# Splitting half B's recurrent matmuls by output columns in an LSTM step

## The chip, the cores and the metric

The kernel runs on one core of a Trainium2 chip. The metric is the time of one execution on the device, in microseconds (us); before the change it is 1897.9 us, the median of 3 runs (1897.48 to 1903.74). About 0.5% is what a measurement of this kernel can tell from no change.

## What is computed

`x` has 8 sequences of 512 steps with 512 features. An LSTM with 512 hidden units is run over it and added to `x`; a convolution over 8 steps, two projections, a linear scan with 64 states and a last projection are run over that sum and added again.

```python
def step(carry, xw_t):                  # xw_t = x[:, t] @ Wx + b
    prev_h, prev_c = carry
    a = xw_t + prev_h @ Wh              # 8 x 2048: gates i, f, o, g
    next_c = sigmoid(f) * prev_c + sigmoid(i) * tanh(g)
    next_h = sigmoid(o) * tanh(next_c)
    return (next_h, next_c), next_h
```

The 512 steps depend on each other, so the time is close to 512 times that of one step.

## The kernel before

**Matmuls (PE).** The 512 hidden units are four chunks of 128. The moving operand is a weight matrix, as a high and a low float16 part (`whh`, `whl` for Wh, `wxh`, `wxl` for Wx); the stationary operand is the state (`stat`, 16 or 32 columns) or the input (`xs`). The outputs are halves: A (output chunks 0 and 1) and B (chunks 2 and 3), each with PSUM tiles `hp[h]` of 128 x 256. Columns 0 to 191 hold gates g, i and f, columns 192 to 255 gate o. One "group" below is the 4 matmuls (L314, q = 0 to 3) of one half, one input chunk and one weight part; they go to four column tiles of the array. A step has 16 such groups. Their order is written out by hand, as (half, input chunk):

```python
PE_ORDER = ((0, 0), (0, 1), (1, 0), (0, 2), (0, 3), (1, 1), (1, 2), (1, 3))
```

Behind them stand the bias (one group, L296) and x's part (`x_mm`, 8 groups, L304) for half t % 2 of the next pair of steps, in another buffer; then at most one or a few float32 matmuls of the second layer, `pl` and `pl2` (L492, L501, L536), from a queue of filler work. Chunks 0 and 1 of `stat` come from half A of the step before, chunks 2 and 3 from half B.

**The order of the rest** is written by hand too. A letter is an operation, the letter after it a half:

```python
ORDER = "TA tA aA gA bA TB vA oA aB gB cA tB kA pA bB oB vB iA mA cB lA kB pB iB mB lB f q E"
```

- `T` (L569, VectorE, "DVE"): long transpose of columns 0 to 191 of `hp` into `Z`. `t` (L572, DVE): short transpose of columns 192 to 255 into `Zo`.
- `a` (L576, DVE): adds the parts of Z into `zp`. `b` (L581, GpSimd, "POOL"): adds the parts of Zo into `zo`.
- `g` (L585, ScalarE, "ACT"): tanh of g, i, f. `o` (L588, ACT): tanh of o, from `zo`.
- `v` (L591), `c` (L595), DVE: the new cell. `k` (L598), `p` (L601), ACT: its tanh and a copy.
- `i` (L604), `m` (L607), `l` (L610), DVE: the new `stat`, high and low part; `l` is what the next step's matmuls wait for.
- `f`: fillers of the second layer on DVE, up to a planned cost FILL = 0.8 a step. `q`: in odd steps a one-column copy on ACT (L657). `E`: fillers on ACT and POOL.

TA is thus the long transpose of half A, lB the last DVE operation of half B. Each engine takes its instructions in this order. `Zo` and `zo` have 4 buffers for each half; a buffer is written again four steps later, and the write has to come after the earlier reads of it: tB after bB of four steps ago (POOL), bB after oB of four steps ago (ACT).

Of the kernel before, what the change touches and what calls it, by code (L numbers as in the profile page):

```python
# [9 lines left out]
F32 = mybir.dt.float32  # L10
# [9 lines left out]
EXP1 = float(1 << 23)  # L20
FMAX = 65504.0

ORDER = "TA tA aA gA bA TB vA oA aB gB cA tB kA pA bB oB vB iA mA cB lA kB pB iB mB lB f q E"

PE_ORDER = ((0, 0), (0, 1), (1, 0), (0, 2), (0, 3), (1, 1), (1, 2), (1, 3))
DUMMY = 4
FILL = 0.8
TAILD = 14
# [62 lines left out]
def lstm_conv_ssm_kernel(ctx: ExitStack, tc: tile.TileContext, xT, condT, wx, wh, brow, cbp, wpp, bpp,  # L91
                         wsp, bsp, alogp, dtlogp, wop, bop, outT):
    nc = tc.nc
    T = xT.shape[2]
# [4 lines left out]
    v, s, pe, sp = nc.vector, nc.scalar, nc.tensor, nc.sync  # L99

    cp = ctx.enter_context(tc.tile_pool(name="cp", bufs=1))
# [5 lines left out]
    wb = [[cp.tile([128, 4, 4, 512], F16, name=f"w{m}{p}") for p in "hl"] for m in "hx"]  # L107
# [3 lines left out]
    def carve(slot, off, shape, parts=128):  # L111
        n = 1
        for d in shape:
            n *= d
        a = wraw[0:parts, slot, off:off + n]
        if len(shape) == 2:
            a = a.rearrange("p (a b) -> p a b", a=shape[0])
        elif len(shape) == 3:
            a = a.rearrange("p (a b c) -> p a b c", a=shape[0], b=shape[1])
        return a  # L120
# [9 lines left out]
    def load_x(n, t0=0, t1=BLK):  # L130
        if n < NBLK:
            sp.dma_start(xbuf[n % 4][:, :, t0 * NB:t1 * NB],
                         xT[:, :, n * BLK + t0:n * BLK + t1, :].rearrange("p k t b -> p k (t b)"))

    seen = cp.tile([128, 1], F32, name="seen")
    v.memset(seen, 0.0)
    s.activation(seen, seen, AF.Tanh)

    seq = [(0, 0), (1, 0), (1, 1), (1, 2), (1, 3), (0, 1), (0, 2), (0, 3)]
# [24 lines left out]
    hp = [[t[:, 0:256] for t in r] for r in hpb]  # L164
# [4 lines left out]
    pool = nc.gpsimd  # L169
# [123 lines left out]
    def bias_mm(P, h):  # L293

        for q in range(4):
            pe.matmul(hp[h][P % 2][32 * q:32 * q + 32, :], bst[P > 0][:, q], bmov[:, 256 * h:256 * h + 256],  # L296
                      start=True, stop=False, tile_position=(0, 32 * q), skip_group_check=True)

    def x_mm(P, h, ks):
        S = xs[P // (BLK // 2) % 2]  # L300
        for k in ks:
            for W in wb[1]:
                for q in range(4):
                    pe.matmul(hp[h][P % 2][32 * q:32 * q + 32, :], S[:, k, P % (BLK // 2)],  # L304
                              W[:, k, q, 256 * h:256 * h + 256],
                              start=False, stop=False, tile_position=(0, 32 * q), skip_group_check=True)

    def h_mm(t, h, ks):
        S = stat[t % 2]
        o = 16 * (t % 2)  # L310
        for k in ks:
            for wi, W in enumerate(wb[0]):
                for q in range(4):
                    pe.matmul(hp[h][(t // 2) % 2][32 * q:32 * q + o + 16, :], S[:, k, 0:o + 16],  # L314
                              W[:, k, q, 256 * h:256 * h + 256],
                              start=False, stop=(k == 3 and wi == 1),
                              tile_position=(0, 32 * q), skip_group_check=True)


# [26 lines left out]
                                  op=ALU.mult),  # L346
# [55 lines left out]
        bias_mm(0, h)  # L402
    for c, (m, k) in enumerate(seq):
        for h in range(2):
            x_mm(0, h, (k,)) if m else h_mm(0, h, (k,))

    cv = carve(0, 0, (4, NT))
    e, w, x = (carve(0, 1024 + 256 * i, (NT,), 64) for i in range(3))
    lt = [[carve(1, 1024 * i + 256 * j, (NT,), 64) for j in range(4)] + [carve(2, 1024 * i, (4, NT))] for i in range(2)]
    fl = Filler(fps)  # L410
# [18 lines left out]
    def add_x(n, t0=0, after=-1):  # L429
        for k in range(4):  # L430
            src, tmp, dst = x_parts(n, k, t0)
            sx = SX[:, k:k + 1]
            a = fl.add("po", lambda k=k, src=src, tmp=tmp: nc.gpsimd.tensor_scalar(
                tmp, src, CL[:, 0, k:k + 1], CL[:, 1, k:k + 1], op0=ALU.min, op1=ALU.max),
                deps=(xlast.get((n - 1, k)),), after=after)
            a = fl.add("xa", lambda sx=sx, tmp=tmp, dst=dst: s.activation(dst[0], tmp, AF.Copy, scale=sx),
                       deps=(a,), after=after)
            xlast[n, k] = fl.add("xd", lambda sx=sx, tmp=tmp, dst=dst: v.scalar_tensor_tensor(
                dst[1], tmp, sx, dst[0], op0=ALU.mult, op1=ALU.subtract), deps=(a,), after=after, cost=0.4)
# [180 lines left out]
    for t in range(T):  # L620
        n, r = divmod(t, BLK)
        if r == 0:
            assert all(h["x2"] in fl.done for h, (b0, *_) in zip(hist, l1blocks) if b0 < t - BLK)
            load_x(n + 2)
            if n + 1 < NBLK:
                add_x(n + 1, 0, t)
        if nl1 < len(l1blocks) and l1blocks[nl1][0] + l1blocks[nl1][1] <= t:
            add_l1(nl1, *l1blocks[nl1])
            nl1 += 1
        if t:  # L630
            for h, k in PE_ORDER:
                h_mm(t, h, (k,))

        P = t // 2 + 1
        if 2 * P < T:
            assert P < 6 or all( xlast[2 * P // BLK, k] in fl.done for k in range(4))
            bias_mm(P, t % 2)
            x_mm(P, t % 2, range(4))
        room = (1 if t < T - 32 else 3) if 2 * P < T else 4
        while room > 0:  # L640
            cost = fl.pop("pl2", t) or fl.pop("pl", t)
            room -= cost
            if not cost:
                break
        ch = {"A": Chain(t, 0), "B": Chain(t, 1)}
        for op in ORDER.split():
            if op == "f":
                left = FILL
                while True:
                    got = fl.pop("xd", t, left) or fl.pop("d2", t, left) or fl.pop("dve", t, left)  # L650
                    left -= got
                    if not got:
                        break
            elif op == "q":

                if t % 2:
                    s.activation(seen, ch["B"].tc[:, 0:1], AF.Copy)  # L657
            elif op == "E":
                for _ in range(2):
                    fl.pop("xa", t) or fl.pop("al2", t) or fl.pop("al", t)  # L660
                fl.pop("po", t)
            else:
                getattr(ch[op[1]], "o_" if op[0] == "o" else op[0])()
        fl.pop("sp", t)
# [69 lines left out]
```

## Time and profile before

| | us |
|---|---|
| median of 3 runs | 1897.9 |
| the profiled execution | 1898.87 |
| its span, first to last instruction | 1897.1 |
| first TA to last TB (L569) | 41.0 to 1859.1 |
| busy: PE, DVE, ACT, POOL | 1653.8, 1648.8, 782.2, 288.2 |
| granted TensorE clock, mean | 0.992 |

Columns of a timeline line: start in us, length in us, engine, line of the kernel, operation, output and input tiles, shape of output and input (for a matmul stationary, then moving operand), number of instructions merged into the line, and in brackets how long the engine had been idle and what ended that. PEld is the load of a stationary operand. A group line has busy time, mean length of one in ns, and idle time ahead of it with its causes. A matmul's length includes the way through the array; matmuls that follow each other start closer than that.

### The profile page before, as it was taken

The numbers are of one execution on the slowest core, as the hardware profiler recorded it, in microseconds if no ns is written. First come the engines' busy times: TensorE is split into PE (matmuls) and PEld (weight loads), VectorE is DVE, ScalarE is ACT, GpSimd is POOL, SyncE is SP. The second block draws the span as 40 slices with busy tenths as digits, with TensorE's granted clock in tenths as the row PEclk, the third lists the DMA queues.
The fourth block names the chain that finished last, engine by engine and source line by source line (L and its number), as shares of the span: only waits on it lengthen the run. The fifth ranks groups of instructions, "written<-read, shape, count | busy, mean of one in ns | idle before, by whom it ended". The sixth has DMA issues, their size and how long they took to land.

```text
span 1897.1 us, 119869 instructions
## 1 busy us (share of the span) xinstructions
PE 1653.8 (87%) x51861; PEld 1364.6 (72%) x51861; DVE 1648.8 (87%) x9137; ACT 782.2 (41%) x4684; POOL 288.2 (15%) x1110
## 2 busy tenths in 40 slices
PE   6888898898988889898898988889898898988896
PEld 4777777777777777777777777777776777777786
DVE  8778889898898989889898898989889898898984
ACT  5544344344434444443444434434443344434342
POOL 1211111111111111111111111111111111111110
PEclk9999999999999999999999999999999999999997
DMA  6000000000000000000000000000000000000000
GB/s 237 4 4 15 4 26 4 4 27 4 26 4 4 27 4 26 4 26 4 4 27 4 26 4 5 26 4 27 4 26 4 4 15 4 15 4 15 4 13 15
DMA packets 21428, 33.52 MB, mean 18 GB/s; under 512 B 2592, under 2 KB 19616, under 8 KB 19872
## 3 DMA queue, kind: packets, MB, share of 16 engines
q1 hardware_dynamic: 20656, 25.71, 4.0%
q8 instruction: 405, 6.64, 1.5%
q14 instruction: 127, 1.04, 0.2%
q10 hardware_dynamic: 240, 0.13, 0.0%
HBM read 17.45 MB, written 8.39 MB: 14 GB/s over the span
## 4 chain that ended last, share of the span: by engine, by line
DVE 50%; PE 31%; ACT 11%; POOL 4%; issue 4%; DMA 0%; ACTq 0%; POOLq 0%; DVEq 0%
PE hp L314 20%; DVE Z L569 16%; DVE wraw L480 7%; DVE zp L576 6%; PE hp L304 5%; ACT gate L585 5%; POOL zo L581 4%; DVE stat L610 3%; DVE stat L604 3%; ACT gate L588 3%; PE fps L501 3%; DVE u L591 3%; DVE Zo L572 3%; ACT tc L598 3%; DVE hb L607 2%
## 5 line engine op out<-in xcount | busy, mean ns | idle before, releaser
L314 PE MATMUL hp<-whh,stat 128*16 128x256 f16 (+1 forms) x16384 | 932.8, 274 | 212.8 <-DVE stat L610 208.4
L314 PEld LDWEIGHTS <-stat 128*16 128x16 f16 x32768 | 777.2, 93 | 443.8 <-DVE stat L610 374.2
L314 PE MATMUL hp<-whl,stat 128*16 128x256 f16 (+1 forms) x16384 | 928.9, 273 | 0.2 <-DVE whl L279 0.2
L585 ACT ACTIVATE gate<-zp 128x48 f32<-128x48 f32 x1022 | 216.2, 212 | 906.1 <-DVE zp L576 903.6
L569 DVE STREAM_TRANSPOSE Z<-hp 128x192 f32<-128x192 f32 x1024 | 391.6, 382 | 111.7 <-PE hp L314 98.4
L304 PE MATMUL hp<-wxh,xs 128*32 128x256 f16 x8192 | 481.6, 273 | 5.5 <-DVE xs L354 5.5
L581 POOL TENSOR_TENSOR zo<-Zo 128x16 f32<-128x16 f32 x1024 | 245.1, 239 | 1571.5 <-DVE zp L576 1092.4
L304 PE MATMUL hp<-wxl,xs 128*32 128x256 f16 x8192 | 481.6, 273 | 0.0
L304 PEld LDWEIGHTS <-xs 128*32 128x32 f16 x16384 | 438.9, 97 | 15.4 <-DVE xs L354 5.7
L588 ACT ACTIVATE gate<-zo 128x16 f32<-128x16 f32 x1022 | 220.6, 216 | 158.1 <-POOL zo L581 141.6
L604 DVE SCALAR_TENSOR_TENSOR stat<-gate,tc 128x16 f16<-128x16 f32 x1024 | 179.5, 175 | 69.0 <-ACT tc L598 0.6
L572 DVE STREAM_TRANSPOSE Zo<-hp 128x64 f32<-128x64 f32 x1024 | 229.9, 225 | 0.0
L576 DVE TENSOR_TENSOR zp<-Z 128x48 f32<-128x48 f32 x1024 | 211.2, 206 | 0.0
L610 DVE TENSOR_TENSOR stat<-hb,stat 128x16 f16<-128x16 f32 x1024 | 179.3, 175 | 17.5
L591 DVE SCALAR_TENSOR_TENSOR u<-gate 128x32 f32<-128x32 f32 x1024 | 175.9, 172 | 20.9 <-ACT tc L598 0.2
L480 DVE SCALAR_TENSOR_TENSOR wraw<-x2b,cond,wraw 128x256 f32<-128x256 f32 (+1 forms) x434 | 188.7, 472 | 4.7 <-ACT wraw L483 4.7
L601 ACT ACTIVATE gate<-zp 128x16 f32<-128x16 f32 x1024 | 188.5, 184 | 0.0
L607 DVE SCALAR_TENSOR_TENSOR hb<-gate,tc 128x16 f32<-128x16 f32 x1024 | 186.3, 182 | 0.0
L598 ACT ACTIVATE tc<-zp 128x16 f32<-128x16 f32 x1024 | 185.2, 181 | 0.4 <-DVE zp L595 0.2
L595 DVE SCALAR_TENSOR_TENSOR zp<-u 128x16 f32<-128x16 f32 x1024 | 177.3, 173 | 0.0
L296 PE MATMUL hp<-bmov,bst 128*32 128x256 f16 x2048 | 144.5, 273 | 0.0
L296 PEld LDWEIGHTS <-bst 128*32 128x32 f16 x2048 | 54.7, 97 | 3.2 <-issue 0.3
(121 smaller groups left out, 739.2 us busy)
## 6 DMA issues: line engine op xcount, KB each, us to landing
x<-in_xT_dram SPq DMA_DIRECT2D x15, 512.0 KB, 4.0
out_dram<-wraw SPq DMA_DIRECT2D x15, 512.0 KB, 4.1
wraw<-in_wh_dram SPq DMA_DIRECT2D x4, 1024.0 KB, 13.7
wraw<-in_wx_dram SPq DMA_DIRECT2D x4, 1024.0 KB, 10.9
x<-in_xT_dram SPq DMA_DIRECT2D x2, 256.0 KB, 12.9
wp<-in_wp_dram SPq DMA_DIRECT2D x1, 256.0 KB, 7.1
out_dram<-wraw SPq DMA_DIRECT2D x1, 256.0 KB, 2.8
out_dram<-wraw SPq DMA_DIRECT2D x2, 128.0 KB, 2.2
```

Source lines behind the costliest of these rows:

```text
L304: pe.matmul(hp[h][P % 2][32 * q:32 * q + 32, :], S[:, k, P % (BLK // 2)], W[:, k, q, 256 * h:256 * h + 256], start=False, stop=False, tile ...
L314: pe.matmul(hp[h][(t // 2) % 2][32 * q:32 * q + o + 16, :], S[:, k, 0:o + 16], W[:, k, q, 256 * h:256 * h + 256], start=False, stop=(k == ...
L480: v.scalar_tensor_tensor(cv[:, k, 0:N], src, cond[:, k, j:j + 1], cv[:, k, 0:N], op0=ALU.mult, op1=ALU.add)
L569: v.transpose(self.Z.rearrange("p g r -> p (g r)"), self.P[:, 0:192])
L572: v.transpose(self.Zo.rearrange("p g r -> p (g r)"), self.P[:, 192:256])
L576: v.tensor_tensor(self.zp[:, 0:48].rearrange("p (g b) -> p g b", b=8), self.Z[:, :, o:o + 8], self.Z[:, :, o + 8:o + 16], op=ALU.add)
L581: pool.tensor_tensor(self.zo.rearrange("p (g b) -> p g b", b=8), self.Zo[:, :, o:o + 8], self.Zo[:, :, o + 8:o + 16], op=ALU.add)
L585: s.activation(self.G[:, 0:48], self.zp[:, 0:48], AF.Tanh, scale=self.inv)
L588: s.activation(self.G[:, 48:64], self.zo, AF.Tanh, scale=self.inv)
L598: s.activation(self.tc, self.zp[:, 48:64], AF.Tanh, scale=0.5)
L604: v.scalar_tensor_tensor(self.S[:, :, 0:8], r8(self.G[:, 48:64]), 1.0, r8(self.tc), op0=ALU.add, op1=ALU.mult)
L610: v.tensor_tensor(self.S[:, :, 8:16], self.hf, self.S[:, :, 0:8], op=ALU.subtract)
```

## The change

Half B's matmuls for input chunks 0 and 3 are split by output columns. Columns 0 to 191 (`b0`, `b3`) stay where they were. Columns 192 to 255 (`o0`, `o3`), with both weight parts, become matmuls of their own in a new place `H` of the order, behind TB. The bias and chunks 0 and 1 of x's part stay ahead of them; chunks 2 and 3 of x's part and the second layer's matmuls come behind them. A new place `R` at the end of odd steps copies one column of `zo` on DVE and one column of the gate tile on POOL.

```diff
-ORDER = "TA tA aA gA bA TB vA oA aB gB cA tB kA pA bB oB vB iA mA cB lA kB pB iB mB lB f q E"
-PE_ORDER = ((0, 0), (0, 1), (1, 0), (0, 2), (0, 3), (1, 1), (1, 2), (1, 3))
+ORDER = "TA tA aA gA bA TB H vA oA aB gB cA tB kA pA bB oB vB iA mA cB lA kB pB iB mB lB f q R E"
+PE_ORDER = ('A0 A1 b0 A2 A3 B1 B2 b3', 'o0 o3')
...
+    seenv, seenp = cp.tile([128, 1], F32, name="seenv"), cp.tile([128, 1], F32, name="seenp")
...
-    def h_mm(t, h, ks):
+    def h_mm(t, seq):
...
-        for k in ks:
-            for wi, W in enumerate(wb[0]):
+        for w in seq.split():
+            h, k, a = int(w[0] != "A"), int(w[1]), slice(192 * (w[0] == "o"), 256 - 64 * (w[0] == "b"))
+            for p in (0, 1) if len(w) == 2 else ("hl".index(w[2]),):
                 for q in range(4):
-                    pe.matmul(hp[h][(t // 2) % 2][32 * q:32 * q + o + 16, :], S[:, k, 0:o + 16],
-                              W[:, k, q, 256 * h:256 * h + 256],
-                              start=False, stop=(k == 3 and wi == 1),
+                    pe.matmul(hp[h][(t // 2) % 2][32 * q:32 * q + o + 16, a], S[:, k, 0:o + 16],
+                              wb[0][p][:, k, q, 256 * h + a.start:256 * h + a.stop],
+                              start=False, stop=(k == 3 and p == 1),
                               tile_position=(0, 32 * q), skip_group_check=True)
...
-            for h, k in PE_ORDER:
-                h_mm(t, h, (k,))
+            h_mm(t, PE_ORDER[0])
...
-            x_mm(P, t % 2, range(4))
-        room = (1 if t < T - 32 else 3) if 2 * P < T else 4
-        while room > 0:
...
+            x_mm(P, t % 2, (0, 1))
         ch = {"A": Chain(t, 0), "B": Chain(t, 1)}
         for op in ORDER.split():
-            if op == "f":
+            if op == "H":
+                if t:
+                    h_mm(t, PE_ORDER[1])
+                if 2 * P < T:
+                    x_mm(P, t % 2, (2, 3))
+                room = (1 if t < T - 32 else 3) if 2 * P < T else 4
+                while room > 0:
...
+            elif op == "R":
+                if t % 2:
+                    v.tensor_copy(seenv, ch["B"].zo[:, 0:1])
+                    pool.tensor_copy(seenp, ch["B"].G[:, 48:49])
```

More of the change, by code (lines that the diff above doesn't have):

```diff
@@ L404, in lstm_conv_ssm_kernel @@
         for h in range(2):
-            x_mm(0, h, (k,)) if m else h_mm(0, h, (k,))
+            x_mm(0, h, (k,)) if m else h_mm(0, "AB"[h] + str(k))
     cv = carve(0, 0, (4, NT))
@@ L637, in lstm_conv_ssm_kernel @@
             bias_mm(P, t % 2)
-            x_mm(P, t % 2, range(4))
-        room = (1 if t < T - 32 else 3) if 2 * P < T else 4
-        while room > 0:
[L641 to L644, printed above, removed]
+            x_mm(P, t % 2, (0, 1))
         ch = {"A": Chain(t, 0), "B": Chain(t, 1)}
         for op in ORDER.split():
-            if op == "f":
+            if op == "H":
[5 more added lines that the diff above has]
+                while room > 0:
+                    cost = fl.pop("pl2", t) or fl.pop("pl", t)
+                    room -= cost
+                    if not cost:
+                        break
+            elif op == "f":
                 left = FILL
```

## The prediction

> **What bounds the kernel now.** I read the page's chain first, then its groups, then one step in the timeline.
>
> ```profile
> DVE 50%; PE 31%; ACT 11%; POOL 4%; issue 4%; DMA 0%; ACTq 0%; POOLq 0%; DVEq 0%
> ...
> L569 DVE STREAM_TRANSPOSE Z<-hp 128x192 f32<-128x192 f32 x1024 | 391.6, 382 | 111.7 <-PE hp L314 98.4
> ```
>
> PE and DVE take turns, and long transposes wait for PE. The timeline of a step from the middle, PE first:
>
> ```profile
> 1002.02 0.29 PE L314 MATMUL hp<-whh,stat 128*32 128x256 f16 x4 [0.64 <-DVE stat L610]
> ...
> 1003.02 0.28 PE L314 MATMUL hp<-whl,stat 128*32 128x256 f16 x4
> ...
> 1003.67 0.28 PE L314 MATMUL hp<-whl,stat 128*32 128x256 f16 x4
> ...
> 1004.65 0.28 PE L304 MATMUL hp<-wxl,xs 128*32 128x256 f16 x4
> ```
>
> These are the first group of the step, A's last, B's last and x's last. 15 pitches lie between the first and B's last: 1.65 / 15 = 0.11 us a group. The same step on DVE, and half B's o gate on POOL and ACT:
>
> ```profile
> 1003.35 0.38 DVE L569 STREAM_TRANSPOSE Z<-hp 128x192 f32<-128x192 f32 x1
> ...
> 1003.79 0.20 DVE L576 TENSOR_TENSOR zp<-Z 128x48 f32<-128x48 f32 x1
> 1004.01 0.38 DVE L569 STREAM_TRANSPOSE Z<-hp 128x192 f32<-128x192 f32 x1
> ...
> 1004.64 0.24 DVE L572 STREAM_TRANSPOSE Zo<-hp 128x64 f32<-128x64 f32 x1
> 1004.92 0.19 DVE L591 SCALAR_TENSOR_TENSOR u<-gate 128x32 f32<-128x32 f32 x1
> 1005.02 0.26 POOL L581 TENSOR_TENSOR zo<-Zo 128x16 f32<-128x16 f32 x1 [0.79 <-ACT tc L598]
> ...
> 1005.31 0.22 ACT L588 ACTIVATE gate<-zo 128x16 f32<-128x16 f32 x1 [0.28 <-POOL zo L581]
> 1005.34 0.17 DVE L610 TENSOR_TENSOR stat<-hb,stat 128x16 f16<-128x16 f32 x1
> ```
>
> TA starts 0.05 after A's last group ends (1003.30); fillers end then too. TB starts 0.06 after B's last group ends (1003.95). Is TB bound by PE or by DVE? TA to tA is 0.31, tA to aA 0.13, and an `a` lets the next instruction start after 0.13 (aB 1004.42, cA 1004.55): DVE alone would have TB 0.57 after TA, but it comes after 0.66. So **PE sets TB**, with 0.09 to spare on DVE. From TB to lA's end (1005.51) DVE issues nearly without a gap, but vB starts 0.28 after tB: it waits for gB, which ends at 1004.88. From lA's end to the next group is 0.06. The loop is: groups until TB 1.99, TB to lA's end 1.50, 0.06; 3.55. Over the run: (1859.1 - 0.66 - 41.0) / 511 = 3.557.
>
> **The change, part by part** (times in us from the step's first group, in one step).
>
> 1. *b0 and b3 in 192 columns.* Four groups shrink. Pitch by columns: no float16 row has fewer than 256. Below stands a float32 row with 64; less one's length (0.231), 8 of them start 0.064 apart. Bounds for a 192-column group: no gain (0.110), or in proportion (0.082). I take proportion. Two groups lie ahead of A's end: TA 1.33 to 1.275. Four lie ahead of TB: 1.99 to 1.88. DVE would be ready at 1.275 + 0.57 = 1.845. Gain **0.109**.
>
> 2. *o0 and o3 behind TB.* They write the tile that TB reads; I take it that they wait for TB. TB ends at 1.88 + 0.38 = 2.26, plus 0.06 (DVE to PE): 2.32. PE is done with bias and half of x at 1.57 + 0.08 + 5 x 0.11 = 2.20, so it stands for 0.12, and x's second half and the fillers behind it. A group of 64 columns: from 0.029 (in proportion, 64/256 x 0.11 plus nothing) to 0.064 (float32 row) or 0.110 (no change). I take 0.029. The first after a wait costs 0.013 more (the first pitch at 1002.02 is 0.12 instead of 0.11). The fourth starts at 2.32 + 0.013 + 0.087 = 2.42; its length is 0.28 less 192 columns' 0.08, so 0.20; plus 0.06: **tB at 2.68**, 0.80 behind TB, where before it was 0.63 behind.
>
> 3. *What the late tB costs.* Behind tB on DVE stands vB. Before, it came 0.91 behind TB, at gB's end. Now it is the later of that and of tB plus tB's issue time: 0.13 (tA to aA) to 0.17 (tB's 0.24 less the 0.07 by which TA's 0.38 exceeds its 0.31). So 0.93 to 0.97: everything to lA comes 0.02 to 0.06 later. I take **0.035**; the wait for gB hid the rest.
>
> 4. *oB.* tB ends at 0.80 + 0.24 = 1.04 behind TB (before: 0.87), bB follows. The copies of R show DVE that POOL has read `Zo`, and POOL that ACT has read `zo`, so tB and bB need to wait for one engine each. What a second wait costs is to be seen in the first steps, where no buffer is used again:
>
> ```profile
> 53.64 0.24 DVE L572 STREAM_TRANSPOSE Zo<-hp 128x64 f32<-128x64 f32 x1
> ...
> 53.96 0.24 POOL L581 TENSOR_TENSOR zo<-Zo 128x16 f32<-128x16 f32 x1 [0.78 <-DVE Zo L572]
> ...
> 1870.27 0.68 PE L492 MATMUL fps<-x2b,ws 128*64 128x64 f32 x8
> ```
>
> There bB starts 0.08 after tB's end, later 0.14 (1004.88 to 1005.02). bB: 1.04 + 0.08 = 1.12, ends at 1.36; oB 1.39 (before 1.30). kB, next on ACT, came at 1.43, held by cB; now cB gives 1.46, and oB's issue (at most the 0.125 from oB to kB) 1.47 to 1.51. So iB, mB and lB come 0.03 to 0.08 later, as late as lA or 0.02 more. The next step's A2 needs lB: lB's end plus 0.06 was 0.61 behind the step's first group, and A2 started at 0.66. Now A2 could start at 0.61, so it is late by 0 to 0.03; I take **0.02**.
>
> 5. *R's DVE copy.* Behind the fillers, ahead of TA, every other step. No row has it; a one-column DVE operation (L260) lets the next start after 0.06. TA has 0.04 to spare before it holds TB, and two fillers end just at TA now, in some 60% of steps: about 0.01 in 30% of steps, 1.5 us in all; from 0 to 0.06 x 256 = 15. POOL's copy stands ahead of idle POOL time (15% busy).
>
> 6. *PE's tail.* x ends 0.144 later in the step (0.12 of waiting, 4 x 0.029 + 0.013 for o, less 0.109). The 166 steps with a second-layer matmul had 0.18 (L501, L536: 110 steps) or 0.23 (L492) of idle PE behind it; with a step shorter by 0.06 as well, the 110 lose 0.02: 2 us. In the last 32 steps, where up to 3 are allowed and PE is late already, some 14 steps lose 0.2: 3 us.
>
> Sum: -0.109 + 0.035 + 0.02 = -0.054 a step; x 511 = -27.6; +1.5 + 2 + 3 = **-21.1**. The profiled execution took 1898.9 (span 1897.1 and 1.8 around it), so 1877.8; the median of the runs is 1.0 lower: **1877**.
>
> **A rule that speaks against it.** Four matmuls merged in one line last 0.28, one alone 0.274, so a group's four start almost together. The Trainium skill, TensorE: Matmul & The Clock Gate, "Wait — 56ns, not 53.3ns?", says that start-to-start never drops below about 25 ns however few the columns. Read for each of the 16 o matmuls, that would be 0.40 instead of 0.12, tB 0.28 later and, as an estimate, +0.23 a step, about 2015; read for each column tile, 0.029 just clears it. The rows speak for the second reading. In step 2, PSUM — Partial Sum Buffer, "PSUM bank collisions raise a hardware error", asks that two engines not touch one bank and quadrant at once, even in different columns; no run here shows it.
>
> **The rivals.**
> - *o's groups don't shrink in proportion (slower).* At 0.064 the fourth starts 0.105 later, so tB 0.105 and vB the same: -0.054 + 0.105 = +0.05 a step, about 1925; at 0.110, -0.054 + 3 x 0.081 = +0.19, about 1995. It decides from a group of about 0.047 on. For it: nothing in the trace shows 8 instructions in 0.03. Against: after the wait at 1002.02 a group's four start within 0.02.
> - *The copies don't free bB (no change).* bB stays 0.14 behind tB: oB 1.45, kB 1.55, lB 0.09 later than lA's shift, A2 0.075 late in place of 0.02: -0.054 + 0.055 = 0 a step, 1898 to 1904 with steps 5 and 6. Against it: the first steps.
> - *o's matmuls don't wait for TB (faster).* PE passes on at 2.20, tB is 0.66 behind TB, vB not late: -0.109 and a little for A2, -0.095, or -49; the 110 steps that PE holds lose 0.06 each, 7, and 4.5 as above: about 1860.
>
> **How the numbers follow.** Forecast 0.50 (its own range 1862 to 1888: steps 3 and 4 near their ends), no wait for TB 0.10, no change 0.17, slower 0.23. Faster by over 0.5% (below 1888.4) 0.60, within 0.17, slower (above 1907.4) 0.23. The range takes in the third rival with the best case of steps 3 and 4, and the slow one's near end: 1850 to 1912.
>
> **What would show it.** In a middle step: TB 1.88 behind the first group; four L314 groups of 64 columns 0.03 apart behind TB; tB 0.80 and vB 0.94 behind TB; bB 0.08 after tB's end. If tB is over 0.87 behind TB, or bB 0.14 after tB, the forecast is wrong.

## The result and the profile after

The changed kernel takes 1909.9 us (median of 5 runs, 1908.85 to 1911.18) beside 1898.8 for the kernel before on the same chip: ratio 1.0054 [1.0042, 1.0066]. It is slower by 0.5%; the forecast was 1877. The result lies inside the stated range of 1850 to 1912, but by luck: the upper end stands there for o groups that don't shrink, and they did. The granted clock is 0.992, as before. The profiled execution took 1911.18, its span is 1909.4. Lines of the changed kernel are numbered 2 or 3 higher: the recurrent groups are L317 (before L314), x's part L306, the long transpose L572, the short one L575, POOL's `b` L584, ACT's `o` L591, `i` L607, `l` L613.

The first line of the chain of waits, by engine, in the changed kernel:

```profile
PE 80%; DVE 17%; issue 2%; ACT 1%; POOL 0%; DVEq 0%; POOLq 0%; ACTq 0%
```

Before, DVE held 50% of it and PE 31%. A share of the chain is no gain or loss by itself, but it says where to look: the matmuls in PE's queue. A step from the middle without a second-layer matmul, in the timeline of the changed kernel:

```profile
1012.13 0.29 PE L317 MATMUL hp<-whh,stat 128*16 128x256 f16 x4 [0.38 <-DVE stat L613]
...
1012.60 0.17 DVE L613 TENSOR_TENSOR stat<-hb,stat 128x16 f16<-128x16 f32 x1
...
1012.82 0.98 PEld L317 LDWEIGHTS <-stat 128*16 128x16 f16 x40 [0.15 <-DVE stat L613]
...
1013.78 0.26 PE L317 MATMUL hp<-whl,stat 128*16 128x192 f16 x4
...
1014.09 0.38 DVE L572 STREAM_TRANSPOSE Z<-hp 128x192 f32<-128x192 f32 x1
...
1014.53 0.21 PE L317 MATMUL hp<-whh,stat 128*16 128x64 f16 x4
...
1014.61 0.21 PE L317 MATMUL hp<-whl,stat 128*16 128x64 f16 x4
...
1014.88 0.25 DVE L575 STREAM_TRANSPOSE Zo<-hp 128x64 f32<-128x64 f32 x1
...
1015.21 0.27 POOL L584 TENSOR_TENSOR zo<-Zo 128x16 f32<-128x16 f32 x1 [0.86 <-DVE Zo L575]
...
1015.43 0.17 DVE L613 TENSOR_TENSOR stat<-hb,stat 128x16 f16<-128x16 f32 x1
```

Read against the forecast: tB comes 0.79 behind TB and bB 0.08 after tB's end, as it said; lA (1015.43) ends 1.51 behind TB, no later than before, where it had 0.035 more. The new thing stands near the start: lB of the step before (1012.60) ends 0.64 behind the step's first group, and PE's load of the next stationary operand then stands 0.15 and starts at 0.69 (the bracket of the PEld line). That is A2, the group that needs half B's state. In the view of all waits this is

```profile
PEld L317 <- DVE stat L613: 304.7, 655, 0.9
...
DVE stat L607 <- ACT tc L601: 109.5, 481, 0.2
```

(us in all, times, longest). The same two in the kernel before:

```profile
PEld L314 <- DVE stat L610: 374.2, 498, 1.0
...
DVE stat L604 <- ACT tc L598: 0.6, 2, 0.4
```

PE's loads waited for `l` about once a step; now they wait 655 times, for less time in all. A second wait has come into some steps while the first has shrunk, so the count shows it and the sum hides it. The second line is half B's `i` waiting for ACT's `k`: hardly ever before, now in most steps.

The time of a step (from its first group to the next step's), by what PE does at its end, summed over the steps:

| steps | mean before | mean after | change in all, us |
|---|---|---|---|
| 310 without a second-layer matmul | 3.546 | 3.523 | -7.1 |
| 56 with L492 (64 columns; L495 after) | 3.563 | 3.716 | +8.5 |
| 56 with L501 (128 columns; L504) | 3.546 | 3.627 | +4.5 |
| 54 with L536 (128 columns; L539) | 3.545 | 3.629 | +4.5 |
| the last 31 | 3.672 | 3.737 | +2.0 |

With the few steps left over, +12.1 us, against -21.1 in the forecast. The steps without a second-layer matmul ("plain" below) gained less than half of the 0.054 expected; those with one lost. The mean of the plain steps mixes two kinds. In 253 of the 310 A2 waits, and their median is 3.529 (before 3.545). In the other 57, 56 of them right behind a step of over 3.56, half B was ready in time: A2 starts at 0.605, TB comes at 1.871, and the median is 3.421. With the same narrow b0 and the same late o0, the step is thus as short as step 1 of the prediction wanted it, if only A2 need not wait.

A smaller part of the loss has no cause in the profile. In five places PE stood 0.28 to 0.94 from one matmul to the next within x's or o's groups. Four of them are long enough for the view of waits, which finds nothing that ended them ("issue"):

```profile
PE hp L306 <- issue: 1.3, 3, 0.5
...
PE hp L317 <- issue: 0.7, 1, 0.7
```

By the starts of the matmuls the five cost 2.7 us in all, four of the five in steps with L495. There is none in the kernel before, and none in the experiments e4, e5, e7 and e8 below; each of the others has one to seven. What stops PE there stays open.

### The profile page after: what moved, and what is told of

The parts are those of the page before. It is cut to its first block, busy times and chain, and to the rows that moved or that the text cites. A ratio compares the mean times of both kernels' runs of the same rounds, so it can differ in the third digit from the quotient of the medians.

```text
span 1909.4 us, 135696 instructions
## 1 busy us (share of the span) xinstructions
PE 1745.6 (91%) x60037; PEld 1383.8 (72%) x60037; DVE 1621.4 (85%) x9393; ACT 756.5 (40%) x4684; POOL 330.6 (17%) x1366
## 4 chain that ended last, share of the span: by engine, by line
PE 80%; DVE 17%; issue 2%; ACT 1%; POOL 0%; DVEq 0%; POOLq 0%; ACTq 0%
PE hp L317 54%; PE hp L306 15%; DVE Zo L575 4%; PE fps L504 3%; PE hp L298 3%; PE fps L539 2%; DVE zp L598 2%; PE fps L495 2%; DVE stat L613 2%; DVE u L594 2%; DVE stat L607 2%; DVE hb L610 2%; DVE Z L572 1%; DVE wraw L526 1%; DVE zp L579 0%
## 5 line engine op out<-in xcount | busy, mean ns | idle before, releaser
L317 PEld LDWEIGHTS <-stat 128*16 128x16 f16 x40944 | 895.3, 93 | 442.8 <-DVE stat L613 304.7
L317 PE MATMUL hp<-whh,stat 128*16 128x192 f16 (+1 forms) x20472 | 1059.3, 253 | 131.6 <-DVE stat L613 129.1
L317 PE MATMUL hp<-whl,stat 128*16 128x192 f16 (+1 forms) x20472 | 1032.4, 251 | 0.8 <-DVE whl L281 0.8
L306 PE MATMUL hp<-wxh,xs 128*32 128x256 f16 x8192 | 520.7, 273 | 5.8 <-DVE xs L357 5.3
L306 PE MATMUL hp<-wxl,xs 128*32 128x256 f16 x8192 | 521.1, 273 | 0.7 <-issue 0.7
L584 POOL TENSOR_TENSOR zo<-Zo 128x16 f32<-128x16 f32 x1024 | 242.5, 237 | 1462.6 <-DVE Zo L575 1124.5
L572 DVE STREAM_TRANSPOSE Z<-hp 128x192 f32<-128x192 f32 x1024 | 390.1, 381 | 95.3 <-PE hp L317 89.3
L306 PEld LDWEIGHTS <-xs 128*32 128x32 f16 x16384 | 406.7, 97 | 11.8 <-DVE xs L357 5.6
L591 ACT ACTIVATE gate<-zo 128x16 f32<-128x16 f32 x1022 | 220.6, 216 | 188.9 <-POOL zo L584 188.6
L607 DVE SCALAR_TENSOR_TENSOR stat<-gate,tc 128x16 f16<-128x16 f32 x1024 | 176.7, 173 | 113.6 <-ACT tc L601 109.5
L575 DVE STREAM_TRANSPOSE Zo<-hp 128x64 f32<-128x64 f32 x1024 | 233.5, 228 | 31.5 <-PE hp L317 0.9
L613 DVE TENSOR_TENSOR stat<-hb,stat 128x16 f16<-128x16 f32 x1024 | 185.8, 181 | 17.5
L598 DVE SCALAR_TENSOR_TENSOR zp<-u 128x16 f32<-128x16 f32 x1024 | 195.4, 191 | 0.0
L601 ACT ACTIVATE tc<-zp 128x16 f32<-128x16 f32 x1024 | 176.5, 172 | 0.2 <-DVE zp L598 0.2
L610 DVE SCALAR_TENSOR_TENSOR hb<-gate,tc 128x16 f32<-128x16 f32 x1024 | 174.1, 170 | 0.0
L669 POOL COPY seenp<-gate 128x1 f32<-128x1 f32 x256 | 47.0, 183 | 79.5 <-ACT tc L601 71.1
```

The source lines that it names most:

```text
L317: pe.matmul(hp[h][(t // 2) % 2][32 * q:32 * q + o + 16, a], S[:, k, 0:o + 16], wb[0][p][:, k, q, 256 * h + a.start:256 * h + a.stop], star ...
L572: v.transpose(self.Z.rearrange("p g r -> p (g r)"), self.P[:, 0:192])
L575: v.transpose(self.Zo.rearrange("p g r -> p (g r)"), self.P[:, 192:256])
L584: pool.tensor_tensor(self.zo.rearrange("p (g b) -> p g b", b=8), self.Zo[:, :, o:o + 8], self.Zo[:, :, o + 8:o + 16], op=ALU.add)
L591: s.activation(self.G[:, 48:64], self.zo, AF.Tanh, scale=self.inv)
L598: v.scalar_tensor_tensor(self.zp[:, 48:64], self.u[:, 1], 0.5, self.u[:, 0], op0=ALU.mult, op1=ALU.add)
```

## The experiments

Theory, from the table and the timeline: the o gate of half B comes later, so lB is later beside lA than I allowed, and A2 waits; and x's second half, now late in PE's queue, pushes second-layer matmuls into the next step. These last matmuls of a step, x's second half and the second layer's, are called PE's tail below. The rival, in short: the extra instructions cost the time, wherever they stand. All medians below are beside 1898.4 to 1899.2 for the kernel before; edits are against the changed kernel unless said otherwise.

**The split without the move** (label e1_split_in_place).

```diff
-PE_ORDER = ('A0 A1 b0 A2 A3 B1 B2 b3', 'o0 o3')
+PE_ORDER = ('A0 A1 b0 A2 A3 B1 B2 b3 o0 o3', '')
```

> The same narrow groups and the same copies as in the changed kernel, but o0 and o3 stand directly behind b3, ahead of TB, the bias and x. Theory (the place costs: PE stands about 0.12 us ahead of o because o waits for TB, which the 166 steps with a second-layer matmul pay; in the others the late tB makes lB late, and A2 waits for it): no stand, tB as early as before, TB again at about 1.99 us behind the first group because it waits for all of B. So all steps close to those of the kernel before, 1896 to 1903 us. Rival (the narrow groups, the 16% more PE instructions or the copies cost the time): as the changed kernel, 1905 to 1912 us.

Measured 1916.7, ratio 1.0092 [1.0078, 1.0106]: above both ranges. Plain 3.572. tB is as early as before the change (0.63 behind TB), but TB is at 2.010 instead of 1.981. The last o group, TB and tB in the timeline of this kernel:

```profile
1002.70 0.20 PE L317 MATMUL hp<-whl,stat 128*16 128x64 f16 x4
...
1002.98 0.38 DVE L572 STREAM_TRANSPOSE Z<-hp 128x192 f32<-128x192 f32 x1
...
1003.61 0.24 DVE L575 STREAM_TRANSPOSE Zo<-hp 128x64 f32<-128x64 f32 x1
```

So cutting four groups into eight has a price of its own, some 0.03 a step. About 0.008 of it is more PE time (four pairs of 0.083 and 0.029 in place of four of 0.110). The rest stands between the last group and TB: a transpose that waits for a group of 256 columns starts 0.334 after that group's start (kernel before), for one of 192 columns 0.309 (changed kernel), for one of 64 columns 0.273 (here). 192 columns fewer bring it 0.06 nearer, not the 0.08 that they take at the pitch of 0.11. Whoever waits for a short group at the end of a row waits 0.02 more than in proportion. The rival has this much right: splitting costs some 13 us where it takes nothing off the path. Another 5 us are in the 56 steps with L495, 3.658 here, for a reason that e4 shows below.

**The copies left out** (e2_no_copies).

```diff
-... mB lB f q R E"
+... mB lB f q E"
```

> The changed kernel without the two one-column copies. Theory (in steps without a second-layer matmul lB decides, through A2): bB waits for two engines again and starts 0.14 instead of 0.08 us behind tB, so oB, kB, iB and lB are 0.06 later and the 310 steps without a second-layer matmul take about 3.59 instead of 3.53 us; the 166 others are held by PE and change little. +19 us, about 1929 us. Rival (the copies themselves cost, 0.06 us on DVE ahead of TA in every second step): faster than the changed kernel by up to 10 us, 1900 to 1908.

Measured 1965.3, ratio 1.0345 [1.0331, 1.0359]. The direction is the theory's, the size is larger: it counted the second wait ahead of bB alone, and tB has one too. Half B's long and short transposes, the last o group and POOL's `b` in the timeline of this kernel, one plain step:

```profile
500.98 0.38 DVE L572 STREAM_TRANSPOSE Z<-hp 128x192 f32<-128x192 f32 x1
...
501.50 0.21 PE L317 MATMUL hp<-whl,stat 128*32 128x64 f16 x4
...
501.85 0.25 DVE L575 STREAM_TRANSPOSE Zo<-hp 128x64 f32<-128x64 f32 x1
...
502.24 0.27 POOL L584 TENSOR_TENSOR zo<-Zo 128x16 f32<-128x16 f32 x1 [0.98 <-DVE u L594]
```

From the last o group to tB it is 0.35 (with the copies 0.27: 1014.61 to 1014.88), and bB stands 0.14 behind tB's end (1015.21 against 1015.13 with them: 0.08). Each instruction that waits for two engines starts 0.06 to 0.08 later than one that waits for one. The trace's instruction records show how: here an EVENT_SEMAPHORE record of the same line stands ahead of tB and waits for PE, 0.800 behind TB in step 301, and tB itself waits for POOL and starts at 0.867; in the changed kernel tB itself waits for PE and starts at 0.795, with no such record. Over the plain steps tB is 0.86 behind TB, lB ends 0.73 behind the next step's first group, A2 starts at 0.78, and the step takes 3.663. So the copies are worth 55 us in this order. The median step is 0.146 longer; lB's end comes 0.150 later behind TB, of which tB's and bB's second waits are 0.07 each and a longer bB 0.02.

**One more group of x ahead of o** (e3_one_more_x).

```diff
             x_mm(P, t % 2, (0, 1))
+            x_mm(P, t % 2, (2,), (0,))
...
-                    x_mm(P, t % 2, (2, 3))
+                    x_mm(P, t % 2, (2,), (1,))
+                    x_mm(P, t % 2, (3,))
```

(The last argument is the weight part; chunk 2's high part moves ahead of `o0`.)

> The changed kernel with one more group of x's part (chunk 2, high part) ahead of o0, so that PE works for 0.11 us of the 0.12 us that it stood there. Theory: the o groups start as before, so steps without a second-layer matmul stay at 3.53 us; the 166 steps with one lose 0.10 us each: 1910 - 16 = 1894 us. Rival (the steps with a second-layer matmul are long for another reason, such as the change between narrow groups and float32 matmuls): no change, 1908 to 1912 us.

Measured 1900.5, ratio 1.0005 [0.9996, 1.0014]: between the two, 9.4 us below the change. The group fills the 0.12 in which PE stood behind TB. Plain steps hardly move (3.528 against 3.523), steps with a matmul of 128 columns fall from 3.627 to 3.545: PE's tail was their loss, and in plain steps PE's tail costs nothing. Steps with L495 fall little, from 3.716 to 3.692. They keep the long lB that e4 shows below, and PE's unexplained stops (1.9 us here).

**o3 alone, with that group** (e4_o3_one_more_x), and **o3 alone** (e5_o3). With only chunk 3 split, b0's groups keep their 256 columns ahead of A2:

```diff
-PE_ORDER = ('A0 A1 b0 A2 A3 B1 B2 b3', 'o0 o3')
+PE_ORDER = ('A0 A1 B0 A2 A3 B1 B2 b3', 'o3')
```

> As the run before, and only chunk 3 is split: b0 is whole again, so that A2 starts 0.67 us behind the first group, and two o groups in place of four stand behind TB. Theory: TB 0.055 us earlier than in the kernel before, tB at 0.74 instead of 0.80 behind TB, lB 0.06 earlier than in the changed kernel, 0.64 with the way to PE, so A2 does not wait; every step about 0.053 us shorter than before, PE just not the bound: about 1872 us. Rival (lB is late for another reason than tB, or splitting has a price of its own): 1890 us or more.

> The changed kernel with chunk 3 alone split (b0 whole), x as in the change, two groups ahead of o3: the kernel of the run at 1882 us without the added x group. Theory (PE's stand ahead of o is paid in steps with a second-layer matmul, and there alone): the 310 steps without one stay at 3.50 us, the 110 with a 128-column one go from 3.50 to about 3.59, the 56 others a little up: 1882 + 10 to 14 = 1892 to 1896 us. Rival (with b0 whole the stand is covered): 1882 to 1885.

Measured 1882.4, ratio 0.9912 [0.9898, 0.9925], and 1894.5, ratio 0.9977 [0.9969, 0.9986]. The second falls into its range. The first lies between theory and rival, 10 us above the one and 8 below the other, but its plain steps show the theory's cause: 3.502, TB at 1.929 (the two narrow groups of b3 bring 0.052), lB's end 0.55 behind the next step's first group, as before the change, and A2 at 0.66 without a wait. Half of the 0.109 is given up here, and the step is shorter than with all of it: with b0 narrow and o0 late, A2's operand is not there in time. (The two go together here; e6 below widens b0 and keeps tB as late.) Plain steps of e5 are the same (3.501); its steps with 128 columns take 3.60 instead of 3.496, again PE's tail. What kept e4 above its forecast are for the most part the steps with L495, 3.614. There, lines of POOL and DVE stand like this:

```profile
385.57 0.59 POOL L436 TENSOR_SCALAR xc<-x,cl 128x256 f32<-128x256 f32 x1
...
385.76 0.42 DVE L613 TENSOR_TENSOR stat<-hb,stat 128x16 f16<-128x16 f32 x1
```

lB takes 0.42 instead of 0.175: it ends with POOL's clamp of x (386.16 and 386.18), which the new copy on POOL has moved back beside it. The copy waits for ACT's `o` of half B, and the clamp stands behind the copy.

**The copies alone** (e7_copies_alone): the kernel before with `R` and nothing else.

> The kernel before, with nothing but the two copies of the odd steps. Theory: bB starts 0.06 us earlier, but kB waits for cB anyway, so ordinary steps stay at 3.55 us. Where the POOL copy (which waits for oB) pushes POOL's clamp of x (0.60 us) back, the clamp runs beside lB, and lB takes 0.42 instead of 0.18 us: 32 steps, 0.24 each, less the 0.06 that iB loses now: 1898.9 + 5 to 8 = 1904 to 1907 us. Rival (the copies cost nothing, lB is long for another reason): 1898 to 1900.

Measured 1898.7, ratio 1.0002 [0.9993, 1.0011]: the rival's no change, and the theory's 1904 to 1907 missed. bB comes 0.06 earlier, but ACT's `k` is then held by cB, so the plain steps and those with 128 columns gain 0.002, 1.0 us in all. lB is long (mostly 0.34) in 31 steps, and the steps with a matmul of 64 columns take 3.598 instead of 3.563: 2 us. Copies that free bB are worth nothing where nobody waits for bB.

**The copies behind the other fillers** (e8_o3_copies_last: e4 so; e9_copies_last: the change so).

```diff
-... mB lB f q R E"
+... mB lB f q E R"
```

> The kernel of the run at 1882 us (o3 alone split, one more x group ahead of it), with the copies behind the fillers of E, so that POOL's clamp of x runs right behind bB again. Theory: lB never takes 0.42 us; 32 steps win 0.2: 1875 to 1877 us. Rival (lB's length has nothing to do with the clamp's place): 1882.

> The changed kernel with nothing but the copies moved behind the fillers of E. Theory: lB never takes 0.42 us. 32 steps win up to 0.2, but half of the steps with the clamp have a second-layer matmul too, where PE holds the step as well: 1909.9 less 4 to 7 = 1903 to 1906 us. Rival: 1910, no change.

Measured 1876.4, ratio 0.9881 [0.9868, 0.9895], the fastest of all, and 1907.0, ratio 1.0042 [1.0028, 1.0056]. Line L613 of e8 by itself, and its chain (columns of the first: times, then shortest, median and longest in ns):

```profile
L613 DVE TENSOR_TENSOR stat<-hb,stat x1024: 161/175/177, 43.5 to 1838.1; 128x16 f16<-128x16 f32 x171
```

```profile
DVE 53%; PE 35%; ACT 5%; POOL 3%; issue 3%; DMA 0%; ACTq 0%; DVEq 0%
```

No `l` is over 0.177 now, and the steps with L495 take 3.522 (e4: 3.614): 5.2 of the 6.0 us between the two. DVE and PE share the chain as in the kernel before. In e9 the same edit takes lB's excess away as well, but only 2.9 us of the time, less than expected: its steps with L495 still take 3.594 at the median, held by PE's tail, and PE's unexplained stops (2.9 us here) raise their mean to 3.65.

**o2 and o3 instead of o0 and o3** (e6_o2o3_copies_last: e8 with this order).

```diff
-PE_ORDER = ('A0 A1 B0 A2 A3 B1 B2 b3', 'o3')
+PE_ORDER = ('A0 A1 B0 A2 A3 B1 b2 b3', 'o2 o3')
```

> Chunks 2 and 3 of half B are split in place of 0 and 3, with one more x group ahead of o2 and the copies behind E. As many narrow groups as in the change, but b0 is whole, so A2 would start at 0.66 us behind the first group with no wait, in place of 0.615. Theory (in steps without a second-layer matmul A2 waits for lB, until 0.70): A2 loses only 0.03 now, TB at 1.91 in place of 1.97, these 310 steps 3.47 us in place of 3.52; the steps with one are held by PE at 3.53. About 1873 us. Rival (the loss in ordinary steps comes from the late tB holding DVE, whichever chunk is split): 3.52 us, 1888 us.

Measured 1886.5, ratio 0.9928 [0.9915, 0.9942]: the rival's number. Half of the theory holds: four narrow groups, none of them ahead of A2, give TB at 1.875 and A2 at 0.66 without a wait. The other half fails: lA's end comes 1.577 behind TB instead of 1.50, and the step takes 3.51. TB is only 0.55 behind TA here, so half A's gates arrive later beside TB, and mA, which starts inside bB, takes 0.22 instead of 0.17. By the rows iA is 0.027 later behind TB than in the changed kernel, and mA's length adds 0.046; no run separates the two. The run still says something of A2: tB is as late here as in the change (0.79 behind TB), and with b0 wide A2 does not wait. Six of PE's unexplained stops, 3.6 us, are in the time too.

**The same in plain steps, o3 alone in the others** (e10_o2o3_or_o3): the order is chosen when the step's second-layer matmul is known.

```diff
...
-            h_mm(t, PE_ORDER[0])
+            order = PE_ORDER[fl.ready("pl2", t) or fl.ready("pl", t)]
+            h_mm(t, order[0])
...
-                    h_mm(t, PE_ORDER[1])
+                    h_mm(t, order[1])
```

(`PE_ORDER` now holds e6's order and e8's; `fl.ready`, new and not shown, tells whether a second-layer matmul is due, without taking it. The rest is e6.)

> As the run before in steps without a second-layer matmul, and in steps with one only chunk 3 is split, so that PE has less to do there. Theory: 3.47 us in the 310 steps, 3.50 us in the 110 with a 128-column matmul: about 1867 us. Rival as before, with the second kind of step at 3.50: 1884 us.

Measured 1881.6, ratio 0.9905 [0.9891, 0.9918], the rival's side again: plain steps 3.513, those with 128 columns 3.498. One split chunk (two groups, its two weight parts) is the best size found. With two, TB comes 0.054 earlier than in e8, and lA's end comes 0.062 later behind TB: the gain goes into half A's chain on DVE.

## Why the prediction was wrong, step by step

Of the 33 us between forecast and result, 9.6 are in the plain steps, 12.9 in the 110 steps with 128 columns, 11.5 in the 56 with L495, 0.7 in the last 31; the copy on DVE, priced at 1.5, cost nothing that shows.

- **Step 1** (narrow groups) was right in its price, 0.083 a pitch. Where A2 does not wait, in the steps in which PE is late for another reason, TA is at 1.274 and TB at 1.873, near the forecast of 1.275 and 1.88. Over the plain steps the median of TB is 1.969 (before 1.981): the 0.109 shrank to 0.012, by step 4.
- **Step 2** was right: o groups are 0.028 to 0.029 apart, and tB comes 0.792 behind TB (forecast 0.80). The rival in which they do not shrink falls.
- **Step 3** was too dear. vB is 0.055 later behind TB, but lA's end comes at 1.500 (before 1.511), not 0.035 later: mA is 0.170 long instead of 0.196, and cB follows it sooner. Before, bB started 0.09 ahead of mA, now they start together. Where mA starts 0.03 to 0.09 inside bB (before, e6, e8), it ends 0.03 after bB and takes 0.196 to 0.216; that this is the cause is argued from their places, no run isolates it.
- **Step 4** is the one that failed. The mechanism is the forecast's own (a late oB, iB held by ACT, lB late, A2 waiting), the size is not. I had lB 0 to 0.02 later beside lA and A2 late by 0.02. iB is 0.083 later behind TB, just beyond the 0.03 to 0.08 that I gave it, and lA 0.011 earlier instead of 0.035 later, so lB's end lies 0.643 behind the next step's first group, before 0.549: +0.094. Somewhat more than half of that miss is step 3's: I had measured lB against an lA that was to move with it. I priced iB by the issue times of a row in which `k` was already waiting for cB, and not by the new chain itself: 0.08 from tB's end to bB, 0.25 for bB, 0.12 from oB to kB. And the narrow b0 asks for A2 at 0.615 instead of 0.66, so A2 starts at 0.697, 0.08 late, plus 0.013 behind the wait.

  What I should have added up is half B's own loop: from A2 to TB, from TB to lB's end, 0.054 to the next A2. In the plain steps of the changed kernel (medians) it is 1.269 + 2.199 + 0.054 = 3.522, and the step takes 3.528. In the kernel before it is 3.486 of 3.545, with 0.06 to spare, in e4 3.440 of 3.499, in e2 3.673 of 3.674. With the upper end of my own 0.03 to 0.08, the forecast's numbers give this loop 1.265 + 2.195 + 0.06 = 3.52, more than the 3.49 that I forecast for the step. e4 shows it from the other side: b0 wide, no o0, no wait, a shorter step.
- **Step 5**: on DVE nothing. "POOL's copy stands ahead of idle POOL time" failed: in the steps with L495 the clamp stood there and moved beside lB. e8 shows its price, 5 us.
- **Step 6** failed in size. Of the 0.18 of idle PE behind a matmul of 128 columns I counted all as room. PE, step with L501 (before) and with L504 (changed kernel), up to the next step's first group:

```profile
447.69 0.70 PE L501 MATMUL fps<-wraw,wp 128*128 128x256 f32 x2
448.40 0.29 PE L314 MATMUL hp<-whh,stat 128*32 128x256 f16 x4
```

```profile
907.00 0.29 PE L306 MATMUL hp<-wxl,xs 128*32 128x256 f16 x4
907.21 0.70 PE L504 MATMUL fps<-wraw,wp 128*128 128x256 f32 x2
907.84 0.29 PE L317 MATMUL hp<-whh,stat 128*32 128x256 f16 x4
```

The float32 matmul started 0.71 ahead of the next step's first group, and now that nothing but PE holds that group, 0.63: only 0.08 was room. x's last group is followed after 0.21 instead of 0.11: some 0.10 goes on the change from four column tiles to one float32 matmul, before the change too. Behind it the same: the last of the two float32 records starts 0.309 ahead of the next step's first group, where float32 records of 256 columns that follow each other (L292, at the kernel's start) are 0.216 apart, so again some 0.09. The Trainium skill, TensorEngine Tiling (Array Packing), "Key Properties", says that changing the tiling mode drains TensorE, and gives no figure; that fits the rows, though no run separates the tiling from the float32. PE's own queue in such a step, with its 0.12 of standing, is thus 3.61, more than the 3.49 that the forecast wanted, and 3.607 to 3.610 is their median. e3 shows the cause: with 0.11 of PE's standing filled, they take 3.545.

The lB that ends with POOL's clamp also has a rule: the Trainium skill, SBUF — State Buffer, "Who interferes with whom", says that a DVE instruction with two SBUF inputs contends with a GpSimd instruction that reads SBUF. Here 0.175 became 0.42 beside a clamp of 0.59. Without these two rules the numbers above stand as measured.

The three rivals of the prediction all fall: o shrank, bB was freed, and o did wait for TB. It came out slower by none of them. Neither sign that was to show the forecast wrong appeared (tB over 0.87 behind TB, bB 0.14 after tB): both look at half B's o gate in its own step, and the loss stands in the next one, at A2, and in PE's tail.

## What to carry to other kernels

When an operation is made to come later because "another wait hid it", follow it through to every consumer, the next iteration's first use of its result too, and ask whether the same change makes that consumer ask for it earlier: here both ends of one slack of 0.06 moved at once. Go round every loop from step to step by itself (half A's, half B's, PE's), and not only the one that sets the time now. Idle time of an engine around a change of kind of work is not all room, so price a moved operation in those steps by the rows on both sides of the change. Move the smallest piece first: two of the four split groups, with one more x group where PE stood and the copies where no one waits behind them, gained 1.2% (e8); all four lost 0.5%, with the x group alone 0.05%, which is no change, and with the copies moved alone 0.4%. No run has o0 and o3 with both; o2 and o3 with both gained 0.7% (e6).

## What the runs showed of the hardware that was not expected

- Sixteen matmuls of 64 columns (four groups) start 0.028 to 0.029 apart by group, so 7 ns by matmul where four column tiles share them; but a transpose that waits for such a group starts only 0.06 nearer to it for 192 columns fewer (0.273 against 0.334 from the group's start).
- A second engine to wait for costs 0.06 to 0.08 on POOL and on DVE alike (a wait record of its own ahead of the operation); a one-column copy ahead of it takes this away.
- The change between four column tiles and a float32 matmul costs some 0.10 on the way in and 0.09 on the way back; no run separates the tiling from the type.
- `l`, a DVE operation of 0.175, takes 0.42 beside a POOL operation of 0.59 and ends with it.
